# Preparations and products of the down and FFN items handed out two by two instead of one by one

## The chip, the core and the metric

The kernel runs on one core of one Trainium2 chip. The metric is the device time of one execution in microseconds (us); the time given is the median of the runs.

## The reference, cut to what matters

```python
# x: 2 x 1024 x 1024, that is 2048 rows of 1024
s = silu(x @ w_gate.T)                    # 2752 columns
_, idx = top_k(-abs(s), 1376)             # per row: the smaller half of |s| ...
s[rows, idx] = 0                          # ... is set to zero
s = s * (x @ w_up.T)
x = layernorm(x + s @ w_down.T)           # "down"
# FFN: weights tiled four times along the input, and a low rank part (rank 2)
lin = lambda x, wq, A, B: x @ tile(wq, (1, 4)).T + 0.5 * (x @ A.T @ B.T)
h = silu(lin(x, w1q, a1, b1)) * lin(x, w3q, a3, b3)      # 2752 columns
x = layernorm(x + lin(h, w2q, a2, b2))
```

## The kernel before

**Tiles and stages.** The 2048 rows are 16 tiles of 128, in four groups of four. All float32 products are made from two parts, a high one (`wh`, `mh`, `fh`, `hh`) and the rest (`wl`, `ml`, `fl`, `hl`), with three matmuls for one: high by high, high by rest, rest by high. In the order of the span:

- gate and up (to about 929 us): the two big projections, L353; the search for the smaller half runs beside them and writes the product `m` (before the mask) and the mask `k` as bytes to memory;
- down (about 929 to 1466 us): for each group, for each of six blocks of the 2752 columns (`DB`: 512, 512, 512, 384, 384, 448 wide), for each of the group's four tiles there is one **down item**, 96 in all. I number them 0 to 95, 24 to a group. The search for the last group's halves, and the low rank products x @ A.T ("dots"), run beside it;
- FFN (about 1466 to 1912 us): for each group eight blocks of 344 columns with four items each (f1), and then four items of the second projection (f2); then the end, to 1925 us.

**A down item** has three parts. Its *load* (`down_load`, L698) issues on SP the transfers of `m` (L710, four buffers in all) and of the mask's bytes `u` (L711, two buffers). At the next item, `masks` (L715 to L720) hands out the mask: ACT casts `u` to `ub` (L724, one buffer), and POOL multiplies `m` by it (L725); for the block of 448, which ends in a half chunk, POOL also splits 64 columns into `cm`. Masks are placed behind `lastp`, the last layernorm's power on POOL (L580). Its *preparation* (`down_prep`, L731) transposes `m` in chunks of 128 on PE (L745, and L747 for `cm`) into a PSUM tile `tp` (two buffers); ACT copies that to `mh` (L749) and DVE makes `ml` (L750), four buffers each. Its *products* (`down_mm`, L770, through `run_ops`, L753) are matmuls of 128x512, two for each of the three kinds and each chunk (L765), into a PSUM pair (three buffers), and one addition on DVE into `acc` (L768). With the last block of a tile, `layernorm` (L568) follows: statistics on DVE (L574 to L578), the power on POOL (L580), the scaling on ACT or DVE, and a store to `x_d`. The first block of a tile loads `acc` from `x`. The weights of a block come with `down_w` (L671), at its first tile: loaded and split by ACT (L173) and POOL (L174), or loaded already split (L684).

**An FFN item** of f1 has no preparation of its own; its products are 14 matmuls of 128x344 (`f1_mm`, L958; L981 to L984), followed by silu on ACT (L987), a product on DVE (L988) and the low rank sums (L990, L992). What it needs per tile, `f1_tile` (L915) and `f1_tile2` (L943) make: a fold of the tile's four quarters on POOL (L927 to L929), a small tile `tl` (L933 to L940), and four transpositions (L949, L951). An f2 item's preparation (`f2_prep`, L1004) has six transpositions (L1026, L1031), copies to `hh` (L1028) and `hl` (L1029); its products are L765 again.

**What sets the order.** `item` (L150) issues the load at once and puts the preparation into a queue q1. While q1 holds more than a1 items, `advance` (L156) takes the oldest, hands out its preparation, puts its products into q2, and then hands out products from q2 until a2 are left. Down items come with a1 = 2, a2 = 3 (L634), f1 items with 2 and 2 (L864), f2 items with 2 and 1 (L874). The first three down items are an exception: their preparations are handed out while gate and up still run, and their products go to q2 directly. Handing out isn't yet the order on an engine: the program is built with a scheduler (`schedule_with_timeline_sim=True`, L1088) that orders the instructions of each engine when they can be ready, with the order of handing out as priority. All engines then run their instructions in that fixed order.

Of the kernel before, what the change touches and what calls it, by code (L numbers as in the profile page):

```python
# [65 lines left out]
class Kern:  # L66
# [83 lines left out]
    def item(self, load, prep, mm, a1, a2):  # L150
        load()
        self.q1.append((prep, mm, a2))
        while len(self.q1) > a1:
            self.advance()

    def advance(self):  # L156
        prep, mm, a2 = self.q1.pop(0)
        prep()
        self.q2.append(mm)
        while len(self.q2) > a2:  # L160
            self.q2.pop(0)()

# [929 lines left out]
```

## Time and profile before

| | |
|---|---|
| median of 3 runs | 1923.47 us (1922.35 to 1924.25) |
| profiled execution | 1926.91 us |
| its span | 1925.1 us |
| mean granted PE clock | 0.993 |
| busy PE, DVE, POOL, ACT | 98%, 64%, 51%, 47% |
| moved by DMA | 488.66 MB, 254 GB/s |

The profile is of one execution: what each engine did, with start, duration, the source line, and the tiles it wrote and read (out <- in). PE is the engine of the matmuls and of the transpositions (matmuls with a unit matrix); DVE, ACT and POOL do elementwise work; SP issues transfers. "Idle before <- releaser" gives how long the engine waited ahead of an instruction and whose end ended the wait. Durations of PE rows overlap, because matmuls are pipelined: the pitch from start to start tells what one costs. The granted clock is the share of its full clock that PE was given.

### The profile page before, as it was taken

The numbers are of one execution on the slowest core, as the hardware profiler recorded it, in microseconds if no ns is written. First come the engines' busy times: TensorE is split into PE (matmuls) and PEld (weight loads), VectorE is DVE, ScalarE is ACT, GpSimd is POOL, SyncE is SP. The second block draws the span as 40 slices with busy tenths as digits, with TensorE's granted clock in tenths as the row PEclk, the third lists the DMA queues.
The fourth block names the chain that finished last, engine by engine and source line by source line (L and its number), as shares of the span: only waits on it lengthen the run. The fifth ranks groups of instructions, "written<-read, shape, count | busy, mean of one in ns | idle before, by whom it ended". The sixth has DMA issues, their size and how long they took to land. (4 is left out here: it accounts for less than half of the span.)

```text
span 1925.1 us, 29381 instructions
## 1 busy us (share of the span) xinstructions
PE 1885.3 (98%) x10825; PEld 1754.4 (91%) x10825; DVE 1229.6 (64%) x1831; ACT 904.0 (47%) x1448; POOL 973.0 (51%) x606
## 2 busy tenths in 40 slices
PE   9999999999999999999999999999998999998998
PEld 9999999999999999999888787888787979898896
DVE  4633556767358574691238998688467857779565
ACT  4333477414883258622246533323333746557362
POOL 5655664445445354355565443554565746436062
PEclk9999999999999999999999999999999999999999
DMA  7677687676977868667798756977776878485651
GB/s 266 237 250 260 236 325 261 210 272 253 330 231 241 314 235 303 236 228 256 282 328 285 270 188 227 337 245 261 268 250 244 279 284 321 155 318 177 229 196 66
DMA packets 166205, 488.66 MB, mean 254 GB/s; under 512 B 24772, under 2 KB 45380, under 8 KB 166056
## 3 DMA queue, kind: packets, MB, share of 16 engines
q1 hardware_dynamic: 165848, 486.43, 71.9%
q8 instruction: 85, 1.39, 0.3%
q14 instruction: 64, 0.52, 0.1%
q10 hardware_dynamic: 208, 0.31, 0.0%
HBM read 370.30 MB, written 116.33 MB: 253 GB/s over the span
## 5 line engine op out<-in xcount | busy, mean ns | idle before, releaser
L174 POOL TENSOR_TENSOR wl<-wr,wh 128x1376 fp32r<-128x1376 f32 (+2 forms) x187 | 566.4, 3035 | 466.1 <-ACT wh L173 436.8
L353 PE MATMUL mm<-wh,xh 128*128 128x344 f32 x1928 | 610.4, 322 | 2.8 <-DMA wh<-tw3T1h 2.8
L353 PE MATMUL mm<-wh,xl 128*128 128x344 f32 x1928 | 609.8, 320 | 0.0
L173 ACT CAST wh<-wr 128x1376 fp32r<-128x1376 f32 (+2 forms) x192 | 232.4, 1215 | 340.9 <-PE mm L353 199.6
L353 PEld LDWEIGHTS mm<-wh,xh 128*128 128x128 f32 x1928 | 364.7, 189 | 3.0 <-issue 3.0
L353 PEld LDWEIGHTS mm<-wh,xl 128*128 128x128 f32 x1928 | 364.6, 189 | 0.0
L353 PE MATMUL mm<-wl,xh 128*128 128x344 f32 x1928 | 342.1, 319 | 0.0
L353 PEld LDWEIGHTS mm<-wl,xh 128*128 128x128 f32 x1928 | 310.1, 188 | 0.0
L765 PE MATMUL mm<-wh,mh 128*128 128x512 f32 x680 | 217.8, 400 | 0.1
L765 PE MATMUL mm<-wl,mh 128*128 128x512 f32 x680 | 215.1, 395 | 1.1 <-POOL wl L174 1.1
L765 PE MATMUL mm<-wh,ml 128*128 128x512 f32 x648 | 205.5, 396 | 0.8 <-DVE ml L750 0.8
L460 ACT ACTIVATE jk<-a,cur 128x2752 int8<-128x2752 f32 x66 | 170.8, 2588 | 31.2 <-DVE cur L482 15.8
L994 POOL TENSOR_TENSOR hf<-hf,gt 128x344 f32<-128x344 f32 x96 | 142.2, 1491 | 75.6 <-DVE gt L988 68.7
L725 POOL TENSOR_TENSOR m<-m,ub 128x512 f32<-128x512 f32 (+2 forms) x93 | 111.0, 1194 | 128.0 <-ACT ub L724 65.8
L981 PE MATMUL mm<-wh,fh 128*128 128x344 f32 x512 | 166.2, 325 | 5.8 <-DVE gt L988 5.2
L983 PE MATMUL mm<-wh,fl 128*128 128x344 f32 x512 | 164.0, 320 | 0.0
L982 PE MATMUL mm<-wl,fh 128*128 128x344 f32 x512 | 163.9, 320 | 0.0
L765 PEld LDWEIGHTS mm<-wl,mh 128*128 128x128 f32 x680 | 127.4, 188 | 30.1 <-POOL wl L174 2.2
L768 DVE TENSOR_TENSOR acc<-acc,mm 128x1024 f32<-128x1024 f32 x96 | 116.4, 1214 | 57.9 <-PE mm L765 27.8
L765 PEld LDWEIGHTS mm<-wh,mh 128*128 128x128 f32 x680 | 124.7, 189 | 24.8 <-ACT mh L749 0.5
L765 PEld LDWEIGHTS mm<-wh,ml 128*128 128x128 f32 x648 | 121.2, 189 | 26.9 <-DVE ml L750 1.0
L992 ACT ACTIVATE pa<-pa 128x344 f32<-128x344 f32 x256 | 123.0, 483 | 38.6 <-DVE pa L990 34.0
(191 smaller groups left out, 2742.5 us busy)
## 6 DMA issues: line engine op xcount, KB each, us to landing
wr<-wu SPq DMA_DIRECT2D x64, 688.0 KB
wr<-wg SPq DMA_DIRECT2D x52, 688.0 KB
wr<-wd SPq DMA_DIRECT2D x48, 512.0 KB
s_d<-cc SPq DMA_DIRECT2D x64, 344.0 KB
m_d<-mt SPq DMA_DIRECT2D x64, 344.0 KB
a<-s_d SPq DMA_DIRECT2D x64, 344.0 KB
wl<-wc_w SPq DMA_DIRECT2D x48, 344.0 KB
wh<-wc_w SPq DMA_DIRECT2D x48, 344.0 KB
```

Source lines behind the costliest of these rows:

```text
L173: self.lasta = self.nc.scalar.copy(hi, raw)
L174: (eng or self.nc.gpsimd).tensor_tensor(lo, raw, hi.bitcast(F), ALU.subtract)
L353: self.nc.tensor.matmul(o, l, r, start=start and n < m and n % (2 * KH) == 0, stop=stop and n >= m and (n - m) % KH == KH - 1)
L460: nc.scalar.activation(jk.bitcast(I8), av[j], AF.Sign, bias=t, scale=-1.0, accum_out=s)
L725: nc.gpsimd.tensor_tensor(m[:, :w], m[:, :w], ub[:, :w], ALU.mult)
L765: nc.tensor.matmul(ps[:, h], a, b[:, h * 512 : (h + 1) * 512], start=i == 0, stop=i == len(ops) - 1)
L768: nc.vector.tensor_tensor(out, out, ps.rearrange("p a b -> p (a b)"), ALU.add)
L981: nc.tensor.matmul(o, fh[:, c, :], wh[:, c, :], start=c == 0, stop=False)
L982: nc.tensor.matmul(o, fh[:, c, :], wl[:, c, :], start=False, stop=False)
L983: nc.tensor.matmul(o, fl[:, c, :], wh[:, c, :], start=False, stop=False)
L992: nc.scalar.activation(pa[:, r], pa[:, r], AF.Copy, scale=0.5, accum_out=part[:, r, b : b + 1])
L994: G.tensor_tensor(hf[:, hs], hf[:, hs], gt, ALU.add)
```

## The change

Two items are taken from q1 in a row, so two preparations are handed out one behind the other, and then the products of as many items as are above a2, which are two. q1 may hold one item more before it happens. That holds for down items and FFN items alike. The final `flush` still goes one by one. 93 of the 96 down items go through `item`; pairs are counted from the fourth.

```diff
     def item(self, load, prep, mm, a1, a2):
         load()
         self.q1.append((prep, mm, a2))
-        while len(self.q1) > a1:
-            self.advance()
-
-    def advance(self):
-        prep, mm, a2 = self.q1.pop(0)
-        prep()
-        self.q2.append(mm)
+        while len(self.q1) > a1 + 1:
+            self.advance(2)
+
+    def advance(self, n=1):
+        for _ in range(n):
+            prep, mm, a2 = self.q1.pop(0)
+            prep()
+            self.q2.append(mm)
         while len(self.q2) > a2:
             self.q2.pop(0)()
```

## The prediction

> **What bounds the kernel now.** I began with the busy times. PE is busy for 98% of the span, so what the change can save on PE is what PE waits, plus what a matmul costs more than it must. Next came the table of PE's waits: it is short, and its rows name the places. The row that the change touches directly is L745 on L725: a transposition of a down item waits for its mask.
>
> ```profile
> PE 1885.3 (98%) x10825; PEld 1754.4 (91%) x10825; DVE 1229.6 (64%) x1831; ACT 904.0 (47%) x1448; POOL 973.0 (51%) x606
> ```
> ```profile
> PE mm L981 <- DVE gt L988: 5.2, 8, 1.7
> PE tp L745 <- POOL m L725: 4.3, 2, 2.7
> PE tp L949 <- POOL fold L929: 3.2, 2, 1.9
> ```
>
> (us in total, times, longest.) Then PE's timeline, row by row. I measure a stall by starts: from the start of one row to the start of the next, less the usual pitch of the matmuls between. The pitch (start to start, median) is 228.5 ns for 128x512, 157 ns for 128x344 and 109 ns for transpositions within a block.
>
> **The change of kind itself: 0.** This is a block of four transpositions among products, and a block of eight:
>
> ```profile
> 1222.43 0.62 PE L765 MATMUL mm<-wh,ml 128*128 128x512 f32 x2
> 1222.89 0.60 PE L745 MATMUL tp<-ident,m 128*128 128x128 f32 x4
> 1223.24 0.70 PE L765 MATMUL mm<-wh,mh 128*128 128x512 f32 x2
> 1223.79 0.40 PE L765 MATMUL mm<-wl,mh 128*128 128x512 f32 x1
> ```
> ```profile
> 1437.33 0.62 PE L765 MATMUL mm<-wh,mh 128*128 128x512 f32 x2
> 1437.79 0.49 PE L745 MATMUL tp<-ident,m 128*128 128x128 f32 x3
> 1438.12 0.27 PE L747 MATMUL tp<-ident,cm 128*128 128x128 f32 x1
> 1438.23 0.49 PE L745 MATMUL tp<-ident,m 128*128 128x128 f32 x3
> 1438.55 0.27 PE L747 MATMUL tp<-ident,cm 128*128 128x128 f32 x1
> 1438.58 0.71 PE L765 MATMUL mm<-wl,mh 128*128 128x512 f32 x2
> 1439.13 0.62 PE L765 MATMUL mm<-wh,ml 128*128 128x512 f32 x2
> ```
>
> From 1222.43 to 1223.79 it is 1.36 us; four products at 0.2285 are 0.914; the four transpositions added 0.446. From 1437.33 to 1439.13 it is 1.80, less 0.914, so eight added 0.886. Over all blocks without a stall the medians are 0.447 and 0.883: about 109 ns per transposition and 10 ns for the change. Two blocks of four made one save 2 x 447 - 883 = 11 ns. If all 96 down items were paired, that is 48 x 11 ns = 0.5 us, which is the most that the stated purpose is worth. It will not reach even that. A scheduler orders each engine's instructions, and the handing out is only a priority to it: in the two programs as built, PE's order has 155 blocks of transpositions before and 154 after. One reason is that mh and ml have four buffers: with two preparations in a row and three products still queued, the second one's mh needs the buffer of an item whose products have not been handed out. I take 0, with 0 to -0.5 as bounds.
>
> So the change is a reordering: transpositions move by up to 10 us of PE work against the products, some masks change places with layernorm's pow on POOL, and the FFN's first transpositions come at other times. What follows prices that. No instruction is added or removed, DMAs included. On SP the loads of m and u keep their order; what moves past them are the loads and stores that the products issue (acc, x_d), by at most one item.
>
> **Masks at the group boundaries: +2.7 in all.** Where a group ends, the layernorms of its four tiles run, and before the change each of the next masks stands on POOL behind one pow (L580), which waits for DVE:
>
> ```profile
> 1192.65 0.55 POOL L580 TENSOR_TENSOR y<-ve,mhalf 128x1 f32<-128x1 f32 x1 [12.91 <-DVE ve L578]
> ```
>
> The mask itself follows at 1193.17 and takes 1.15 us. Meanwhile on PE:
>
> ```profile
> 1191.06 0.62 PE L765 MATMUL mm<-wh,mh 128*128 128x512 f32 x2
> 1194.38 0.66 PE L745 MATMUL tp<-ident,m 128*128 128x128 f32 x4 [2.70 <-POOL m L725]
> ```
>
> PE lost 3.32 - 0.457 = 2.86 us there (item 49; I count the down items 0 to 95, 24 to a group). In the program after, the masks of items 25, 49 and 73, and of 27, 51 and 75, are ahead of the pow that they stood behind; 26, 28, 50, 52, 74 and 76 are not.
> *Group 1.* Item 27's stall of 1.46 us (1072.40) goes, since its mask is freed. Next late is item 28: its mask ended 0.84 us before its transpositions, they are asked for 1.6 us of PE work earlier, and everything is 1.46 earlier: 1.6 + 1.46 - 0.84 = 2.2 us of new wait. Sum +0.7.
> *Group 2.* Item 49's 2.86 goes. Item 50 had 0.27 us to spare and is asked for 0.5 later, so it now waits 2.86 - 0.27 - 0.5 = 2.1. Sum -0.8.
> *Group 3.* Item 82 (1374.12) already lost 1.79 us: ACT was held for 5.28 us by the issue of L813's transfers ahead of the cast of u (L724). That order stays, and the transpositions are asked for 3.4 us earlier: +3.4. The next stalls, 1.51 at 1379.86 (L949 on the fold) and 0.66 at 1389.21 (wl of L174), are absorbed by it: -2.2. But the stall becomes 1.79 + 3.4 = 5.2 us, and after long stalls the granted clock is half for 3.413 us at a time, in this trace after stalls of 2.96, 2.98 and 3.56 us. In such a stretch the 128x512 pitch is 427 ns, so 3.413 x (1 - 229/427) = 1.58 us are lost; I take 1.55. Sum +2.8.
> Below, the masks could cost nothing and the stalls go; above, if no mask comes earlier, items 25, 49 and 73 are asked for 6.7, 4.5 and 4.6 us before their masks' ends.
>
> **End of down and the first FFN tiles: -7.25.** The last item's products follow transpositions that come late:
>
> ```profile
> 1457.91 0.55 PE L745 MATMUL tp<-ident,m 128*128 128x128 f32 x3 [1.17 <-DVE fl L955]
> 1458.30 0.27 PE L747 MATMUL tp<-ident,cm 128*128 128x128 f32 x1
> 1459.34 1.22 PE L765 MATMUL mm<-wh,ml 128*128 128x512 f32 x2 [0.77 <-DVE ml L750]
> ```
>
> Two products started at 1456.12: 1.79 - 0.457 = 1.33 to the first row. 1458.30 to 1459.34 less one pitch is 0.93, and 0.37 more follow: 2.65 us in all, with a half clock stretch after. In the new order item 93's products follow its own transpositions 0.1 us later, so about one trip through ACT and DVE stays: I leave 1.3, so -1.35, and -1.55 for the stretch. Then the transpositions of four FFN tiles are bunched:
>
> ```profile
> 1477.43 0.38 PE L951 MATMUL tp<-ident,tl 128*128 128x128 f32 x2
> 1477.96 0.44 PE L949 MATMUL tp<-ident,fold 128*128 128x128 f32 x2
> 1478.78 0.41 PE L951 MATMUL tp<-ident,tl 128*128 128x128 f32 x2 [0.38 <-DVE tl L940]
> 1481.06 0.44 PE L949 MATMUL tp<-ident,fold 128*128 128x128 f32 x2 [1.87 <-POOL fold L929]
> ```
>
> 0.30 + 0.55 + 2.04, and 0.67 between the last L951 and the L981 behind it, are 3.56 us lost, then a half clock stretch. In the new order these four stand 9.4, 2.2, 6.6 and 13.2 us of PE work later, with products between: I leave 0.8, so -2.8, and -1.55 again. Cover for all this are the L981 products that move ahead; if they are not ready, up to the whole 7.25 stays.
>
> **Rest of the FFN: +1.3.** The order differs by a few us only. ACT waits 1.16 and 1.50 us for weights there (L173, 1517.11 and 1525.21); a PE that arrives earlier meets the same transfers. I give back half of these 2.66 us; bounds 0 and 2.7.
>
> Clock rule: the Trainium skill ("TensorE: Matmul & The Clock Gate", "Why this matters for your kernels") asks for no PE idle gap over about 3 us. Here the row of 2.86 at 1191 kept the full clock, 2.65 in pieces did not: by the rule alone only one of the two stretches that I remove would be removable. The same page ("Part 4: PE-mode transpose") speaks against the change: transpositions do not count as busy for the clock. The blocks of eight at 1437.79 and 1452.13 ran at full granted clock, so I price that at nothing.
>
> **Sum.** 0 + 0.7 - 0.8 + 2.8 - 1.35 - 1.55 - 2.8 - 1.55 + 1.3 = -3.25, about -3.2 us. The profiled execution took 1926.91 us (span 1925.1, 1.8 around it), 3.4 above the median 1923.47. So 1923.7 for it, and 1920.3 for the median.
>
> **Rivals.**
> *Slower: the transpositions pulled ahead wait for masks that are no earlier.* Place: item 54 (asked for 4.3 us before its mask's end) and one of 25, 49 and 73 (mean 5.3). -3.2 + 4.3 + 5.3 = +6.4: 1929.9. For it: 23 of the 93 masks that are handed out this way had under 1.1 us to spare, so masks run just in time. Against: those three are freed of a pow in the new order, and u of item 54 is issued ahead of the acc loads behind which it landed 9 us late. It decides once the new waits exceed 3.2 us, and measurably at 7.1.
> *Faster: all these stalls go and none returns.* 1.46 + 2.86 + 1.79 + 1.51 + 2.65 + 3.56 + 2 x 1.55 = 16.9: 1906.6. Against: each boundary has a second mask behind a pow, and item 82 is asked for earlier.
> *The change does only what it says, or nothing:* 0 to -0.5: 1923.0. Against: the order after differs all through the down stage.
>
> **Chances.** Forecast 0.40, slower rival 0.30, faster rival 0.15, nothing 0.15. About 0.2% (3.85 us) is what a measurement of this kernel can tell from no change. The forecast lies near that bound: half of it counts as faster. Faster 0.20 + 0.15 = 0.35; same 0.20 + 0.15 and 0.03 of the slower rival = 0.38; slower 0.27. The range takes in the forecast (with 0 to 2.7 given back, and one clock stretch kept), most of the slower rival and the near half of the faster: 1910 to 1932.
>
> **What would show it.** PE's blocks of transpositions near 154; no stall at item 49, but one of about 2 us at items 28 and 50, and about 5 at item 82 with a half clock stretch; no bunch of L949 and L951 with 3.5 us of waits after down, and two half clock stretches fewer there. It is wrong if items 25, 49, 54 or 73 wait for L725, or if the FFN's stalls on L988 (5.2 us now) grow.

## The result, and the profile after

| | before | after |
|---|---|---|
| median | 1922.91 us (1921.53 to 1924.25, 4 runs) | 1932.74 us (1929.3 to 1933.83, 4 runs) |
| ratio | | 1.005, 95% interval 1.0035 to 1.0065 |
| profiled execution, its span | 1926.91, 1925.1 us | 1933.83, 1930.9 us |
| mean granted PE clock | 0.993 | 0.991 |

The change makes the kernel about 9.8 us slower. All line numbers of after are one higher from the changed function on: L745 is L746, L949 is L950, and so on. The work is the same, and so is PE's share; these are the busy row and the first rows of PE's waits (us in total, times, longest) after:

```profile
PE 1888.7 (98%) x10825; PEld 1757.4 (91%) x10825; DVE 1230.9 (64%) x1831; ACT 905.9 (47%) x1448; POOL 972.6 (50%) x606
```
```profile
PE mm L982 <- DVE gt L989: 6.4, 9, 1.7
PE tp L746 <- POOL m L726: 5.9, 2, 5.7
PE tp L950 <- POOL fold L930: 4.5, 2, 2.3
PE mm L766 <- ACT hh L1029: 4.5, 3, 3.0
```

The wait for a mask, 4.3 us in two before (longest 2.7), is now nearly all one wait of 5.7. PE's order as it ran has 154 blocks of transpositions, against 155 before (the kernel's opening run of 128x128 matmuls, L117, counted as one); among products of 128x512 there are 22 of three (30 before), 67 of four (71), and ten of six to eight (four). Most items are not paired on PE.

**Where the time went.** PE's work has the same amount in both, so I cut it into stretches by amount of work, at usual pitches, and take the time by which each stretch lasted longer than its work: its lost time. The stretches are named by the times they have in the profile of before. The numbers are worked out from the starts of PE's matmuls in each trace, one execution each; "second" is another profiled execution of the same kernel, taken with the experiments (`before_2` at 1922.82 us, `after_2` at 1928.75 us).

| lost us in the stretch | before | before, second | after | after, second |
|---|---|---|---|---|
| 1068 to 1370.5, boundaries of groups 1 and 2 | 7.2 | 6.2 | 5.8 | 4.9 |
| 1370.5 to 1384, item 82 in group 3 | 3.4 | 1.0 | 8.5 | 6.6 |
| 1384 to 1476, rest of down | 7.1 | 5.7 | 9.7 | 5.9 |
| 1476 to 1580, the FFN's first part | 14.0 | 14.8 | 14.8 | 16.4 |

The four rows add up to 7.1 us more after than before in the first two executions, and 6.1 in the second two. The spans of these executions differ by 5.8 and 6.0 us, less than the 9.8 of the medians, so the traces show most of the loss and not all of it.

The waits at the boundaries of groups 1 and 2 go, as the change's order of masks would have it: after, PE has no stall over 0.25 us from 1030 to 1297. (A new one of 1.66 us follows at 1297.11, not in `after_2`.) Group 3 takes back far more. First item 82. On PE, in the trace of after:

```profile
1369.03 0.62 PE L766 MATMUL mm<-wh,ml 128*128 128x512 f32 x2
1375.35 1.11 PE L746 MATMUL tp<-ident,m 128*128 128x128 f32 x4 [5.70 <-POOL m L726]
1376.12 1.20 PE L766 MATMUL mm<-wh,mh 128*128 128x512 f32 x2
```

and on ACT at the same time:

```profile
1365.86 2.63 ACTq L814 DMA_DIRECT2D br<-braw  x2
1368.59 0.59 ACT L750 CAST mh<-tp 128x512 fp32r<-128x512 f32 x1 [4.45 <-DMA u<-k_d]
1371.40 1.95 ACTq L814 DMA_DIRECT2D br<-braw  x2
1373.39 0.62 ACT L725 CAST ub<-u 128x512 bf16<-128x512 uint8 x1 [4.22 <-DMA wr<-wd]
```

The cast of u (L725), which the mask waits for, stands behind four issues of br's small transfers, until 1373.39. The issues themselves take 1.18, 0.58, 0.57 and 0.57 us. The rest of the time ACT waits ahead of them: by the semaphore events of the trace, until transfers that SP had issued before have landed, of u at 1367.89 and of weights at 1371.33 and 1372.76 (L712, L685, L604). Eight semaphores are used in turn, and each of these issues goes out only when the transfer that had its semaphore before is there. Products at 1376.12 then start 1.00 us apart for two (1376.12 to 1377.12), where 0.457 is usual: the clock is half there. The end of down and the FFN's first tiles follow:

```profile
1452.95 0.62 PE L766 MATMUL mm<-wl,mh 128*128 128x512 f32 x2
1455.76 0.57 PE L950 MATMUL tp<-ident,fold 128*128 128x128 f32 x2 [2.19 <-POOL fold L930]
1456.12 0.63 PE L952 MATMUL tp<-ident,tl 128*128 128x128 f32 x2
1456.55 0.85 PE L746 MATMUL tp<-ident,m 128*128 128x128 f32 x3
1457.19 0.42 PE L748 MATMUL tp<-ident,cm 128*128 128x128 f32 x1
1458.29 1.22 PE L766 MATMUL mm<-wh,mh 128*128 128x512 f32 x2 [0.68 <-ACT mh L750]
```
```profile
1483.33 0.38 PE L952 MATMUL tp<-ident,tl 128*128 128x128 f32 x2
1486.06 0.44 PE L950 MATMUL tp<-ident,fold 128*128 128x128 f32 x2 [2.35 <-POOL fold L930]
1486.33 0.38 PE L952 MATMUL tp<-ident,tl 128*128 128x128 f32 x2
```

Where before waited 1.17 and 0.77 us (1457.91 and 1459.34), after waits 2.19 for a fold, then 0.68 for mh. Of the bunch of FFN tiles two still stand back to back. Between them POOL makes the second one's fold:

```profile
1483.63 0.72 POOL L928 TENSOR_TENSOR fold<-x2a 128x256 f32<-128x256 f32 x1 [3.25 <-issue]
1484.46 0.73 POOL L929 TENSOR_TENSOR fold<-fold,x2a 128x256 f32<-128x256 f32 x1
1485.27 0.74 POOL L930 TENSOR_TENSOR fold<-fold,x2a 128x256 f32<-128x256 f32 x1
```

From start to start PE loses 2.51 us there, where before lost 0.55 and 2.04 in a row. After each of the three places the granted clock is half; the windows of these stretches of after (us, busy times of PE, its weight loads, DVE, ACT and POOL, then clock, DMA share, GB/s):

```profile
1374.20:1380.90 6.70, 5.55 (x15) 4.55 (x16) 2.51 (x3) 2.02 (x4) 5.92 (x8) 0.50 0.60 202
1456.20:1462.90 6.70, 6.03 (x22) 4.90 (x21) 5.57 (x16) 1.76 (x3) 4.54 (x8) 0.51 0.81 293
1486.90:1490.20 3.30, 3.30 (x12) 3.30 (x13) 3.30 (x7) 2.51 (x8) 3.22 (x5) 0.52 0.89 312
```

### The profile page after: what moved, and what is told of

Its sections match the earlier page's. It is cut to its first block, busy times and chain, and to the rows that moved or that the text cites. A ratio compares the mean times of both kernels' runs of the same rounds, so it can differ in the third digit from the quotient of the medians.

```text
span 1930.9 us, 29377 instructions
## 1 busy us (share of the span) xinstructions
PE 1888.7 (98%) x10825; PEld 1757.4 (91%) x10825; DVE 1230.9 (64%) x1831; ACT 905.9 (47%) x1448; POOL 972.6 (50%) x606
```

## The experiments

My theory after the result: the order makes PE ask for transpositions sooner than what they need is there, in group 3 and at its end. The rivals: the FFN items' pairs cost; the deeper queue costs, not the pairs; it is one place (item 82, behind ACT's issues); it is chance of how pairs fall. Each kernel was timed against the kernel before on the same chip, whose median lay between 1921.8 and 1923.6 us. Intervals are 95%; a second value in parentheses after a time is the ratio.

**What a change of kind costs (`kind`).**

```diff
+            z, zo = self.wh.get()[:, :512], self.pair()
+            nc.gpsimd.memset(z.bitcast(F), 0.0)
+            nc.scalar.copy(z[:, 0:P], self.ident)
+            for reps, prod, tps in ((24, 8, 4), (12, 16, 8), (1, 192, 96), (96, 2, 1), (48, 4, 2), (6, 32, 16)):
+                for _ in range(reps):
+                    for i in range(prod):
+                        nc.tensor.matmul(zo[:, i % 2], z[:, 0:P], z, start=True, stop=True)
+                    for i in range(tps):
+                        nc.tensor.transpose(warm[:, i % 4, :], self.ident, self.ident)
             self.gate_up()
```

> The kernel before with 2304 added matmuls ahead of its first stage, whose results nobody reads: 192 products of 128x512 and 96 transpositions in each of six patterns, in turns of 8 products and 4 transpositions, 16 and 8, 192 and 96, 2 and 1, 4 and 2, 32 and 16. If a change of kind costs about 10 ns, as the blocks in the trace of before say, 24 turns and 12 turns differ by 0.1 to 0.2 us, and 96 turns of 2 and 1 cost about 1 us more than one turn. If a change of kind were dear (0.1 us or more, the reason for which one would pair items), 24 against 12 turns would differ by 1.2 us or more and the 96 turns by about 10 us.

(The added matmuls are 6 x 288 = 1728; 2304 was a miscount.) One execution. The windows of the six patterns, 24 turns of 8 and 4, 12 of 16 and 8, one of 192 and 96, 96 of 2 and 1, 48 of 4 and 2, 6 of 32 and 16:

```profile
14.51:69.43 54.92, 54.92 (x292) 45.46 (x290) 11.72 (x4) 1.62 (x2) 8.32 (x2) 1.00 0.26 90
69.43:123.86 54.43, 54.43 (x291) 45.97 (x290) 0.00 (x0) 0.00 (x0) 0.00 (x0) 1.00 0.00 1
123.86:177.89 54.03, 54.03 (x291) 46.48 (x290) 0.00 (x0) 0.00 (x0) 0.00 (x0) 1.00 0.00 1
177.89:232.94 55.05, 55.05 (x292) 41.99 (x290) 0.00 (x0) 0.00 (x0) 0.00 (x0) 1.00 0.00 1
232.94:287.99 55.05, 55.05 (x290) 44.35 (x289) 0.00 (x0) 0.00 (x0) 0.00 (x0) 1.00 0.00 1
287.99:342.19 54.20, 54.20 (x291) 46.25 (x290) 0.00 (x0) 1.34 (x1) 0.00 (x0) 1.00 0.00 1
```

From 24 turns to 12 saves 0.49 us, 40 ns for each two turns merged, four times my 11 ns. But 96 turns cost 1.02 us over one, 11 ns a turn, as I expected, and 48 turns take as long as 96. So the price lies between 11 and 40 ns, by the patterns that are compared. Part of the 0.49 is no change of kind: from product to product the median pitch is 231 ns in the first pattern and 227 in the second. At the highest price all 48 mergings would save 48 x 40 ns = 1.9 us, half of what can be told from no change. A change of kind is cheap.

**Which items (`d_only`, `g012`, `g3`, `g3b`, `not3b`).** The edit is the same, with another condition each:

```diff
-        while len(self.q1) > a1 + 1:
-            self.advance(2)
+        n = 2 if self.dgr < 4 else 1
+        while len(self.q1) > a1 + n - 1:
+            self.advance(n)
```

`dgr` is the group whose down items are handed out, 4 and more in the FFN; in `g012` the condition is groups 0 to 2, in `g3` group 3, in `g3b` column blocks 4 and 5 of group 3, in `not3b` all down items but these.

> Pairs for the down items alone; the FFN items go one by one as before. Theory (the loss comes from waits in the down stage's last group and at its end): about as slow as the change, +5 to +10 us. Rival (the FFN items' pairing costs): within 2 us of before.

> Pairs for the down items of groups 0 to 2 alone; group 3 and the FFN go one by one. Theory (the two waits of 1.46 and 2.86 us at the first two group boundaries go, a new one of 1.66 comes at 1297, and all the loss lies in group 3 and behind it): 1.5 to 4 us faster than before. Rival (the waits in group 3 are tied to transfers that come no earlier, so a PE that arrives earlier only waits longer): within 1 us of before. Rival (pairing costs wherever it is): slower by 3 us or more.

> Pairs for the down items of group 3 alone. Theory (all of the loss comes from group 3, with the end of down and the FFN's first tiles): as slow as the change, +8 to +12 us. Rival (the loss is a sum over all groups, with the order that groups 0 to 2 leave behind): +1 to +5 us.

> Pairs for the last eight down items of group 3 alone (column blocks 4 and 5). Theory (the loss is the 5.9 us wait for the mask of item 82, with the half clock behind it, in column block 2): within 2 us of before. Rival (the loss is the end of down, where the transpositions of the FFN's first tiles wait for their fold): +4 to +9 us.

> The change without its last part: pairs for all down items but the last eight of group 3; the FFN goes one by one. Theory (two places cost: about 5 us at the last eight items, as pairing these alone cost, and about 5 us at item 82 of group 3 when all groups are paired): +4 to +6 us. Rival (all is given back or lost at the end of down, whatever comes before it): within 2 us of before.

| kernel | median us | ratio, interval |
|---|---|---|
| d_only | 1932.73 | 1.0061, 1.0048 to 1.0074 |
| g012 | 1921.93 | 1.0000, 0.9991 to 1.0010 |
| g3 | 1928.98 | 1.0031, 1.0021 to 1.0042 |
| g3b | 1928.26 | 1.0028, 1.0016 to 1.0039 |
| not3b | 1927.02 | 1.0019, 1.0009 to 1.0030 |

The FFN's pairs are no part of it: without them the loss is whole (10.9 us, just above the theory's range). (Pairs for the FFN alone weren't run.) Pairs in groups 0 to 2 change nothing, although their boundary waits are gone in `g012`'s trace: 3.5 us are lost there, 7.2 and 6.2 in the two executions of before. At item 82 it loses 2.7 where these lost 3.4 and 1.0. The time is what the first rival of `g012` expected; where the gain at the boundaries went isn't shown. Pairs in group 3 alone cost about 6 us, between the two expectations of `g3`; in its last eight items alone 5, everywhere but there 4.

The last two, 1.0028 and 1.0019, make nearly the 1.005 of the change. Another cut doesn't add up: groups 0 to 2 alone and group 3 alone, 1.0000 and 1.0031, make only half of the 1.0061 of `d_only`, and the intervals of `g3` and `d_only` stand apart. So pairs in the first groups, which cost nothing by themselves, raise the price of those in group 3. Item 82 shows it in the traces: it waits about 5 us with both (`d_only`, `not3b`), while `g3` loses only 1.2 us in its stretch. How the one brings the other isn't shown.

**Depth or pairs (`depth`, `pair0`).** `depth` keeps `while len(self.q1) > a1 + 1` and calls `self.advance()`; `pair0` is

```diff
-        while len(self.q1) > a1 + 1:
+        while len(self.q1) > a1:
             self.advance(2)
```

> The queue of preparations may hold one item more, as in the change, but items are handed out one by one. Theory (pairing moves transpositions against masks, depth alone delays all by one item and gives each mask one item more of time): the waits for masks at the boundaries go, and the time is 0 to 5 us under before. Rival (the depth is what costs, since more transfers and buffers are held ahead): as slow as the change, +6 to +10 us.

> Pairs without the deeper queue: two items are taken as soon as three wait, so that the second of a pair is prepared one item sooner after its load than before. Theory (transpositions that are asked for sooner than their masks are what costs): slower than the change, +12 to +25 us above before, with waits for L726 at many items. Rival (depth costs, pairs don't): within 3 us of before.

`depth`: 1925.5 us (1.002, 1.0011 to 1.003), between the two expectations: the deeper queue costs about 4 us by itself. `pair0`: 1940.56 us (1.0088, 1.0073 to 1.0103), in the range of the theory. Its waits:

```profile
PE mm L766 <- ACT mh L750: 6.0, 5, 2.3
PE tp L746 <- POOL m L726: 5.1, 5, 2.1
PE mm L766 <- ACT hh L1029: 4.7, 3, 3.0
```

Five waits for masks and five for mh, and its groups 1 and 2 lose 13.7 us where after loses 5.8 and before 7.2. So pairs at before's depth cost about 17 us, and one item more of depth takes back some 7 of them. My reading is that the pair's second item is asked for too soon; the depth in the change is then a mend for its pairs, and the mend isn't whole.

**Second profiles (`before_2`, `after_2`).** These are the two kernels unchanged.

> The kernel before once more, for a second profile: its first profiled execution was 3.4 us above the median. If that profile is typical, the waits of 1.46 us at 1072, 2.86 at 1191, 1.79 at 1374 and 3.56 at 1477 come again within 0.5 us. If waits of this size change from one execution to the next, some are gone or new ones stand elsewhere, and differences of 1 to 3 us between two single profiles say nothing.

> The change once more, for a second profile. If the wait at item 82 (5.9 us) and the wait for the fold at the end of down (2.3 us) belong to the kernel's order, they come again within 1 us at the same items; if they are accidents of one execution, they don't.

In `before_2` the stall at 1072 came again (1.47 us), that at item 49 was 1.93 instead of 2.86, that at item 82 was not there, and no half clock followed the end of down. So part of the waits that I reckoned with belong to the one execution that I predicted from, not to the kernel. In `after_2` item 82 waited 4.92 us, near the 5.87 of the first, but the fold at the end of down only 0.76. Item 82's wait belongs to the order; it was 5.0 in `d_only` and 4.7 in `not3b` too.

**Item 82 (`a_sp`, `b_sp`, `not3b_sp`, then `a_gp`, `b_gp`, `not3b_gp`).** The small transfers of br go out from SP, or from POOL, instead of ACT:

```diff
-                nc.scalar.dma_start(self.br[w + 2 : w + 4, bs].bitcast(F), lo[w + 2 : w + 4, :].bitcast(F))
+                nc.gpsimd.dma_start(self.br[w + 2 : w + 4, bs].bitcast(F), lo[w + 2 : w + 4, :].bitcast(F))
```

with `nc.sync` in the first three; `a_` is the change with it, `b_` the kernel before with it.

> The change, with the small transfers of br issued by SP instead of ACT. Theory (ACT is held by these issues while the cast of u for item 82 waits behind them): the wait of 5.9 us at 1369 falls under 2 us, the half clock behind it goes, and the time is 4 to 8 us under the change. Rival (the cast waits for u itself, or SP's queue now holds back the loads behind these transfers): within 2 us of the change, or slower.

> The same, with the small transfers of br issued by SP instead of ACT, which took the wait at item 82 from 5.9 to 1.4 us in the change. Theory of two places: within 2 us of before, since neither place is left. Rival (what is taken away at item 82 is given back at the end of down also with items one by one there): as the kernel without SP, +4 to +6 us.

> The kernel before with the small transfers of br issued by SP instead of ACT. If ACT's hold at item 82 costs before as well (1.79 us in its first profile, none of that size in its second), 0 to 2 us under before; if SP's queue pays for it, 1 to 4 us above.

> The change, with the small transfers of br issued by POOL, so that neither ACT nor SP issues them. Theory (item 82's wait of about 5 us comes from ACT, which these issues hold, and the time it takes away shows once SP doesn't pay): the wait at 1369 under 2 us, and 3 to 6 us under the change, +4 to +7 above before. Rival (whatever is saved at item 82 is waited for at the end of down, which is tied to the FFN's first weights): as the change, +8 to +11.

> Pairs for all down items but the last eight, with the small transfers of br issued by POOL. Theory of two places: both are gone, within 2 us of before. Rival: +4 to +6 us, as with the transfers on ACT.

> The kernel before with the small transfers of br issued by POOL: the price of that edit by itself. If POOL has room (51% busy), within 2 us of before, or up to 2 us under it where ACT's hold cost before too; if POOL's issues delay the masks, 2 to 6 us above.

| transfers of br from | before | change | all but the last eight |
|---|---|---|---|
| ACT | 1 | 1.005, 1.0035 to 1.0065 | 1.0019, 1.0009 to 1.0030 |
| SP | 1.0028, 1.0017 to 1.0039 | 1.0037, 1.0024 to 1.0050 | 1.0044, 1.0028 to 1.0059 |
| POOL | 0.9986, 0.9976 to 0.9997 | 1.0044, 1.0029 to 1.0059 | 1.0009, 0.9998 to 1.0020 |

SP costs 5 us by itself, so the first three told little (item 82's wait fell to 1.4 us in `a_sp`, and the time hardly followed). With POOL, the theory of item 82 falls: in `a_gp` its wait is gone (0.1 us lost there, against 8.5 and 6.6), yet the time is as the rival expected, 1931.78 us. The rest of down lost 16.4 us instead of 9.7 and 5.9, with the granted clock half for 6.83 us from 1435.64 and again from 1452.71. This is the end of down in `a_gp`, PE, then ACT, then some rows of DVE:

```profile
1448.54 0.38 PE L950 MATMUL tp<-ident,fold 128*128 128x128 f32 x2
1448.76 0.38 PE L952 MATMUL tp<-ident,tl 128*128 128x128 f32 x2
1448.98 0.49 PE L746 MATMUL tp<-ident,m 128*128 128x128 f32 x3
1449.30 0.27 PE L748 MATMUL tp<-ident,cm 128*128 128x128 f32 x1
1450.56 0.72 PE L766 MATMUL mm<-wh,mh 128*128 128x512 f32 x2 [0.98 <-ACT mh L750]
1451.12 0.63 PE L766 MATMUL mm<-wl,mh 128*128 128x512 f32 x2
1455.06 0.87 PE L746 MATMUL tp<-ident,m 128*128 128x128 f32 x3 [3.30 <-DVE fl L956]
```
```profile
1448.10 1.44 ACT L174 CAST wh<-wr 128x688 fp32r<-128x688 f32 x2 [5.82 <-DMA wr<-w]
1449.44 0.57 ACT L955 CAST fh<-tp 128x512 fp32r<-128x512 f32 x1
1449.92 0.58 ACT L750 CAST mh<-tp 128x512 fp32r<-128x512 f32 x1
```
```profile
1449.97 1.61 DVE L939 COPY tl<-dr 128x2 f32<-128x2 f32 x1
1452.45 1.27 DVE L575 BATCH_NORM_STATS2 bn<-acc 128x6 f32<-128x512 f32 x2
1453.65 0.85 DVE L175 TENSOR_TENSOR wl<-wr,wh 128x688 fp32r<-128x688 f32 x1
1454.50 0.41 DVE L956 TENSOR_TENSOR fl<-tp,fh 128x256 fp32r<-128x256 f32 x1
```

ACT waits for an FFN weight until 1448.10 and casts it before it copies the tp tiles; the two tp buffers are full, and the next transpositions wait 3.30 us for DVE's fl to free one. Of that wait ACT is not the last cause: its fh is done at 1450.01, and DVE comes to fl 4.5 us later, behind the small tiles tl, a layernorm's statistics and a weight's split. In `b_gp` the same weight lets ACT go at 1447.04, nearly the same time, but there PE has other products to go on with, its longest wait at this place is 0.75 us (1453.28), the clock is full, and the kernel loses 0.5 us at item 82 and 5.5 in the rest of down. The edit gains 1.4 in 1000 before, and 0.6 and 1.0 with the pairs: no more where item 82 waited than where it didn't. (`not3b_gp` is 1.4 us above before, as the theory of two places expected; but against `b_gp`, the same edit without pairs, its ratio is 2.3 in 1000 higher, no less than `not3b`'s 1.9.) So item 82 is a place where the loss stands, not its cause.

**How the pairs fall, and the best of both (`par3`, `g012_gp`).**

```diff
         n, ea = 0, []
+        if g == 3:
+            self.advance()
```

for `par3`; `g012_gp` joins `g012` and POOL's transfers.

> The change, with one item handed out alone at the start of group 3, so that the pairs of group 3 straddle the other way. If the loss belongs to how the pairs of group 3 happen to fall against masks and the FFN's first tiles, it changes by 3 us or more, either way; if it belongs to pairing as such, the time stays within 2 us of the change, +8 to +12 above before.

> Pairs for groups 0 to 2 alone, and br's small transfers issued by POOL: both edits that cost nothing or gained by themselves (0.0 and -2.7 us). If the 2 to 3 us that the pairs save at the boundaries of groups 1 and 2 are lost again in group 3 whatever stands there, -1 to -4 us; if ACT's hold was what took them back, -4 to -7 us.

`par3`: 1931.15 us (1.0047, 1.0028 to 1.0066). Its pairs straddle the other way and its waits stand elsewhere (3.87 us for a fold at 1374, 3.40 for mh at 1412, none for item 82's mask), but the time is the same: of the two ways in which the pairs can fall neither is better. `g012_gp`: 1920.01 us (0.9987, 0.9977 to 0.9996), as `b_gp`: the gain at the first boundaries doesn't come through even then. Both are 2 to 3 us faster than before, and faster than the change by about 12.

## Why the prediction was wrong, step by step

The forecast was 1920.3 us, the range ended at 1932; it was 1932.74, and slower, not faster.

The lost time of PE in the places of the sum tells which step failed (us, cut as above; the last column is from the second executions):

| | forecast | after less before | second |
|---|---|---|---|
| 1068 to 1331, groups 1 and 2 | -0.1 | -2.2 | -3.1 |
| 1331 to 1440, group 3 | +2.8 | +5.4 | +5.5 |
| 1440 to 1500, end of down and first FFN tiles | -7.25 | +2.2 | +1.7 |
| 1500 to 1912, rest of the FFN | +1.3 | +0.9 | +1.2 |

- **Change of kind, 0:** the price per merging was between 11 and 40 ns, my 11 at its low end, and the reading held: there is one block less (154), and all 48 mergings would be worth 1.9 us at most.
- **Groups 1 and 2, +0.7 and -0.8:** better in the traces (the new waits at items 28 and 50 didn't come), but worth nothing in time: `g012` stands at 1.0000. Item 27's stall, which I put down to its mask, ends in the trace of before with DVE's ml (L750), 0.39 us after the mask: it waited for a tp buffer as well.
- **Group 3, +2.8:** item 82 was right in place and size, 5.87 us against 5.2 forecast, and the half clock behind it came, two windows long instead of one. The two stalls that were to be absorbed (1.51 and 0.66 us) are gone in the trace of after. The step was too small by 2.6 us: the longer wait, the second window, and smaller waits beside it.
- **End of down and first FFN tiles, -7.25:** this is the step of the sum that failed, by 9 us, nearly all that parts the forecast from the result in the traces. Both half clock stretches that it took away stayed: one from 1455.93, two windows long, one from 1486.65. I moved transpositions away from their waits and left the producers where they were. But the fold has one buffer: the next tile's fold can only be made when the last one's is transposed. Two tiles stand back to back in the new order too, and between them PE waits for three POOL instructions of 0.73 us: 2.51 us from start to start (ahead of 1486.06), where before lost 0.55 + 2.04. A wait that is a loop PE - POOL - PE doesn't shrink when all of it moves later. It stands at the start of the FFN in every trace, with pairs or without: as 2.51 us in eight of the 20, as 0.55 and 2.04 in eleven, in other pieces in `pair0`. The 2.19 us ahead of 1455.76 have another cause: there POOL had to leave the same buffer to DVE's L660 (until 1453.29), which computes dots and throws its output into it. That the buffer is the reason in both places is read from the rows and the code; no run gave the fold a second one.
- **Rest of the FFN, +1.3:** about right; the waits on L989 (6.4 us against 5.2; 5.9 against 5.6 in the second executions) grew.
- **The base:** I subtracted waits of one execution, 3.4 us above the median, from the median. The second execution hadn't two of those that I reckoned with: the half clock at 1459, a gain of 1.55 us that wasn't always there to be had, and the 1.79 at item 82, by which I took its new wait for an increase of 3.4 when it can be one of the whole 5.
- **The slower rival** had a mechanism that the rows bear out, transpositions pulled ahead of what they wait for, and the wrong places: item 54 and items 25, 49 and 73 didn't wait. It put the decision at masks; in group 3 PE waits for ACT's and DVE's copies and the fold as well. That its 1929.9 us lie near the result is luck.
- **The clock:** the Trainium skill ("TensorE: Matmul & The Clock Gate", "Why this matters for your kernels") warns of idle gaps over about 3 us. Here 2.51 us from 1483.44 were enough, while 2.86 at item 49 before were not. The same page ("Part 4: PE-mode transpose") says that transpositions don't count as busy for the clock; in `kind` 96 of them in a row, some 10.5 us (96 x 109 ns), ran at a granted clock of 1.00, so the measurement differs, and that rule played no part.

Shown by runs: without pairs of down items in group 3 there is no loss, with the FFN's pairs no part of it; pairs there alone make about half of it, and the rest comes only together with pairs in the groups before; depth without pairs costs 4 us and pairs without depth 17; neither ACT's hold at item 82 nor the way in which the pairs fall makes it. Not settled: the mechanism, that is, what ties the end of group 3. The rows point to ACT's order there (FFN weights cast ahead of mh) and to DVE's (fl behind other work), with two tp buffers and one for the fold; but no run took any of that away, and a third tp buffer wasn't tried.

## What to carry to other kernels

A regrouping is priced first by what a change of kind costs (here 11 to 40 ns, from 1728 added matmuls), and by whether the built order groups anything at all; what then remains is a shift of when each engine is asked, and a pipeline that runs just in time pays for asking sooner. A wait may only be struck from a sum with its producer traced: if the producer itself waits for the engine that waits, or lands at the same time whatever PE does, the wait moves along. Before microseconds are taken from one profile, a second one of the same kernel tells which of the waits come again.

## What the runs showed of the hardware

- The granted clock changes only on a fixed grid: in all 20 traces every half clock stretch starts a whole multiple of 3.413 us after the first one and lasts one or two such steps, but for the last, which runs on past the kernel's end (before: starts at 0, 15, 169, 176 and 197 steps). In line with that, a longer stall may bring none and a shorter one may: 2.86 us (item 49) did not, 2.04 (second execution of before, at 1473.81, with 0.54 just ahead of it) did.
- Issuing DMAs of 2.7 KB isn't free for an engine in a tight place: the 16 issues took ACT 0.57 to 1.18 us each in after, and ahead of them it waited for earlier transfers of another engine to land (2.2 us before 1371.40). From POOL, 51% busy over the span, they made the kernel before 0.14% faster; from SP, 0.28% slower.
- Single executions of one kernel differ by 7 to 10 us from lowest to highest (before on one chip: 1918.24 to 1925.42 in 23 runs; one run of 3102.91 on another chip left out), so a loss of 4 us was told from about a dozen runs.
